# Expert blocks at fixed places, with a scatter that adds weighted rows into the output

## Chip, cores and metric

The kernel runs on one core of one Trainium2 chip. The metric is the device time in microseconds (us), the median over runs; lower is better. Engines are named as in the profile: PE (TensorE), DVE (VectorE), ACT (ScalarE), POOL (GpSimd) and SP (SyncE, which here only issues transfers).

## What is computed

Two layers act on 4 x 32 x 32 tokens of 256 channels, 4096 tokens in all. Layer 0 (a convolution and a state-space scan) is not touched by the change. Layer 1 is an attention without softmax and then a mixture of 16 experts, of which each token uses two:

```python
t = t + _L1_attn_ref(_ln_t(t), ...)
t = t + _L1_ffn_ref(_ln_t(t), ...)

def _L1_ffn_ref(x, gate_w, gate_b, w1, w2, w3):      # 256 -> 512 -> 256, 16 experts
    probs = jax.nn.softmax(einsum('bsd,de->bse', x, gate_w) + gate_b, axis=-1)
    top_probs, top_idx = jax.lax.top_k(probs, 2)
    top_probs = top_probs / jnp.sum(top_probs, axis=-1, keepdims=True)
    dispatch = jnp.sum(one_hot(top_idx, 16) * top_probs[..., None], axis=-2)
    hidden = silu(einsum('bsd,edh->bseh', x, w1)) * einsum('bsd,edh->bseh', x, w2)
    expert_out = einsum('bseh,eho->bseo', hidden, w3)
    return einsum('bseo,bse->bso', expert_out, dispatch)
```

So there are 8192 pairs of a token and an expert. With the given inputs the experts get 411, 318, 424, 490, 591, 836, 278, 654, 596, 645, 718, 547, 389, 510, 475 and 310 of them. In blocks of 128 rows (each expert's last block partly empty) that is 73 blocks. Every expert fills or begins at least three, and 25 blocks lie beyond the third of their expert.

## The kernel before

All matrices are float32. The kernel works in four stages.

**Layer 0** takes the first 2720 us or so. It ends on POOL's products `h<-h,cb_n` and DVE's scans.

**Attention** (about 2720 to 2970 us) works through four batches of 8 tiles of 128 tokens. The program is written under a manual schedule: the source order is the order on each engine. In the loop over `o` the work of batch `o` is interleaved with the first part of batch `n = o + 1` and with the gating of batch `z = o - 1`. `out(o, i)` finishes tile i of batch `o` in `t_all`, which holds all 4096 rows of the residual in SBUF. `expert_in(o, half)` normalises four tiles and stores them in `xd` in DRAM. `turn_e` transposes them on PE, `gates` multiplies by the gate weights, and `turn_g` turns the scores back to rows. `route(z)` is a generator: `on_with(steps, n)` runs its next n steps of DVE work in gaps between other work. It picks the two experts (`hot_all`), their weights (`wts`), counts pairs by expert (`counts`), and gives each pair its block within the expert (`within`) and a one-hot code of its place in that block (`qh`). For the last batch this runs with nothing beside it.

**Ordering** (about 2979 to 3001 us). From the final counts each expert gets as many blocks as it needs, one expert after the other: `end` and `first` are the bounds, `eid` the expert of each of up to 79 blocks. Comparisons of every pair's block with all 79 block numbers, and 64 PE products with `qh` (L1742), list for each slot which pair sits in it. From that come `src` (the row of `xd` to gather) and `dst` (the row of `yd` to write; pair 2t + k is row 2t + k, and empty slots go to spare rows).

**Experts** (about 3002 to 3443 us). `blocks_of(0, NFULL)` runs a fixed number of blocks, 74. A branch runs five more if the counts need them. For each block, `fetch_in` reads the expert's number from `eid` on SP (`value_load`), loads `w1` and `w2` (512 KB each) and issues POOL's indirect gather of 128 rows; `fetch_out` loads `w3`. Both run four blocks ahead. `turn_rows` transposes the rows, `hidden` makes two halves of the hidden layer, and `result` multiplies by `w3`. `put_result` copies PSUM to `yb` on DVE, and POOL scatters it:

```python
            yb = ffn.tile([P, C], F32, name="yb", bufs=4)
            nc.vector.tensor_copy(yb, on["pf", i])
            nc.gpsimd.indirect_dma_start(
                yd[:, :], bass.IndirectOffsetOnAxis(dst[:, i : i + 1], 0), yb, None
            )
```

All scatters write one tensor, so the framework makes each wait for the one before. An expert's weights are loaded again for each of its blocks.

**Final sum** (about 3443 us to the end). `yd` is read back in eight parts of 1 MB, DVE adds both rows of each token times their weights to `t_all` (L1879), and ACT's queue stores the output.

Of the kernel before, what the change touches and what calls it, by code (L numbers as in the profile page):

```python
# [16 lines left out]
P = 128  # L17
# [16 lines left out]
def conv_ssm_attn_moe_kernel(ctx: ExitStack, tc: tile.TileContext, a: dict, out: bass.AP):  # L34
# [19 lines left out]
    NBLK = 2 * NB * L // BS + NE - 1  # L54
    assert 2 * NS == P
# [1048 lines left out]
    wts = l1.tile([P, 2, NTA], F32, name="wts")  # L1104

    t_all = l1.tile([P, NTA, C], F32, name="t_all")
    xd = dram.tile([NB * L, C], F32, name="xd")

    yd = dram.tile([2 * NB * L + P, C], F32, name="yd")
# [4 lines left out]
    groups_f = l1.tile([P, NTA], F32, name="groups_f")  # L1114

    places = l1.tile([P, BS], BF16, name="places")
    blocks_h = l1.tile([P, NBLK], BF16, name="blocks_h")

    groups = l1.tile([P, NTA], BF16, name="groups")
    part_pk = l1.tile([P, 2], F32, name="part_pk")  # L1120
    spare = l1.tile([P, 1], F32, name="spare")
# [11 lines left out]
    def constants(first):  # L1133
# [6 lines left out]
        if first:  # L1140
            count(iota, NE, NE)
            make_upper_triangular(nc, before, 1.0, diag=False)
            count(places_f, BS, 0)
            count(blocks, NBLK, 0)
            count(groups_f, NTA, 0)
            count(part_pk, 2, 1, 1, 2)
            count(spare, 1, 2 * NB * L + 1, 1, 1)
            count(block_p, 1, 0, 1, 1)
        else:
            nc.vector.memset(every, 1.0)  # L1150
            nc.vector.memset(keep, 1.0)
            nc.vector.memset(keep[:, :, 0:1], 0.0)
            nc.vector.tensor_copy(places, places_f)
            nc.vector.tensor_copy(blocks_h, blocks)
            nc.vector.tensor_copy(groups, groups_f)

    with tc.tile_pool(name="wa", bufs=1) as wa, tc.tile_pool(name="att", bufs=1) as att, \
# [4 lines left out]
        tbs = [t_all[:, b * NT : (b + 1) * NT, :] for b in range(NB)]  # L1162
        for i in (0, HT):
            nc.sync.dma_start(out=tbs[0][:, i : i + HT, :], in_=rows(td, 0)[:, i : i + HT, :])
# [101 lines left out]
        def fourth(b, i):  # L1266
            on = batch[b]
            junk = sm.tile([P, C], F32, name="junk", bufs=1)
            nc.scalar.activation(
                junk, on["sq"][:, i, 0, :], AF.Square, accum_out=on["q4"][:, i : i + 1]  # L1270
            )
# [124 lines left out]
        def expert_in(b, half):  # L1396
# [14 lines left out]
            nc.sync.dma_start(out=rows(xd, b)[:, lo:hi, :], in_=on["xe"][:, lo:hi, :])  # L1411
# [24 lines left out]
        def route(b):  # L1436
# [18 lines left out]
            first = sm.tile([P, NT], F32, name="first")  # L1455
            hot = [h[:, b * NT : (b + 1) * NT, :] for h in hots]
            for k, top in enumerate((m1, m2)):
# [7 lines left out]
                nc.vector.tensor_reduce(first, cand, AX.X, ALU.min)  # L1465
                yield
                nc.vector.tensor_tensor(hot[k], cand, over_last(first, NE), ALU.is_equal)
# [19 lines left out]
            for k, top in enumerate((m1, m2)):  # L1487
                nc.vector.tensor_tensor(
                    wts[:, k, b * NT : (b + 1) * NT], top, both, ALU.mult
# [31 lines left out]
            )  # L1521
            yield
            for k in range(2):
# [4 lines left out]
                yield  # L1528

# [32 lines left out]
        for o in range(NB):  # L1562
# [24 lines left out]
            turn_next(0)  # L1587
            v_out(o, 0)
# [70 lines left out]
            if n is not None:  # L1659
                fourth(n, NT - 1)  # L1660
                k2(n, 1)
            out(o, 5)
# [5 lines left out]
            out(o, 7)  # L1668
            if n is None:
# [14 lines left out]
    eid = l1.tile([1, NBLK], I32, name="eid")  # L1684

    used_i = l1.tile([P, 1], I32, name="used_i")
    NFULL = 2 * NB * L // BS + NE // 2 + 2
    src = l1.tile([P, NBLK], I32, name="src")
    dst = l1.tile([P, NBLK], I32, name="dst")
    wp = ctx.enter_context(tc.tile_pool(name="wp", bufs=6))  # L1690
    with tc.tile_pool(name="rt", bufs=1) as rt, tc.tile_pool(name="rt2", bufs=3) as rt2, \
            tc.tile_pool(name="ps_r", bufs=1, space=PSUM) as ps_r:

        nbi = rt.tile([P, NE], I32, name="nbi")
        nc.vector.tensor_scalar(nbi, counts[-1], float(BS - 1), None, ALU.add)
        nc.vector.tensor_single_scalar(nbi, nbi, BS.bit_length() - 1, ALU.arith_shift_right)
        nb = rt.tile([P, NE], F32, name="nb")
        nc.vector.tensor_copy(nb, nbi)
        end = rt.tile([P, NE], F32, name="end")
        nc.vector.tensor_tensor_scan(end, every[:, :NE], nb, 0.0, ALU.mult, ALU.add)  # L1700
        nc.vector.tensor_copy(used_i, end[:, NE - 1 :])
        first = rt.tile([P, NE], F32, name="first")
        nc.vector.tensor_tensor(first, end, nb, ALU.subtract)

        pick = rt.tile([P, 2 * NTA, NE], F32, name="pick")
        nc.vector.tensor_tensor(
            pick, hot_all.rearrange("p k g e -> p (k g) e"), over_middle(first, 2 * NTA), ALU.mult
        )
        bf = rt.tile([P, 2, NTA], F32, name="bf")
        nc.vector.tensor_reduce(bf.rearrange("p k g -> p (k g)"), pick, AX.X, ALU.add)  # L1710
        bh = rt.tile([P, 2, NTA], BF16, name="bh")
        nc.vector.tensor_tensor(bh, bf, within, ALU.add)

        done = rt.tile([P, NE], F32, name="done")
        nc.vector.tensor_scalar(done, end, block_p, None, ALU.is_le)
        ef = rt.tile([P, 1], F32, name="ef")
        nc.vector.tensor_reduce(ef, done, AX.X, ALU.add)
        pe = ps_r.tile([1, P], F32, name="pe")
        nc.tensor.transpose(pe, ef, ident)
        nc.vector.tensor_scalar(eid, pe[:, :NBLK], float(NE - 1), None, ALU.min)  # L1720

        pgp = ps_r.tile([P, 2, NBLK], F32, name="pgp")
        GC = NTA // 2
        n = 0
        for k in range(2):
            for c in range(NTA // GC):
                gs = slice(c * GC, (c + 1) * GC)
                ih = rt2.tile([P, GC, NBLK], BF16, name="ih", bufs=2)  # L1730
                nc.vector.tensor_tensor(
                    ih, over_middle(blocks_h, GC), over_last(bh[:, k, gs], NBLK), ALU.is_equal
                )
                both = rt2.tile([P, GC, 2, NBLK], BF16, name="both", bufs=2)
                nc.vector.tensor_tensor(
                    both[:, :, 0, :], ih, over_last(groups[:, gs], NBLK), ALU.mult
                )
                nc.scalar.activation(
                    both[:, :, 1, :], ih, AF.Copy, scale=part_pk[:, k : k + 1]
                )  # L1740
                for j in range(GC):
                    nc.tensor.matmul(  # L1742
                        pgp.rearrange("p s n -> p (s n)"), qh[:, k, c * GC + j, :],
                        both[:, j, :, :].rearrange("p s n -> p (s n)"),
                        start=(n == 0), stop=(n == 2 * NTA - 1),
                    )
                    n += 1
        low = rt.tile([P, NBLK], F32, name="low")
        nc.vector.tensor_copy(low, pgp[:, 1, :])
        pm = rt.tile([P, NBLK], F32, name="pm")  # L1750
        nc.vector.scalar_tensor_tensor(
            pm, pgp[:, 0, :], 2.0 * P, low, ALU.mult, ALU.add
        )
        none = rt.tile([P, NBLK], F32, name="none")
        nc.vector.tensor_scalar(none, pm, 0.0, None, ALU.is_equal)
        row = rt.tile([P, NBLK], F32, name="row")
        nc.vector.scalar_tensor_tensor(row, none, spare, pm, ALU.mult, ALU.add)
        nc.vector.tensor_scalar(dst, row, -1.0, None, ALU.add)
        both = rt.tile([P, NBLK], I32, name="both_i")
        nc.vector.tensor_scalar(both, pm, 1.0, -1.0, ALU.max, ALU.add)  # L1760
        nc.vector.tensor_single_scalar(src, both, 1, ALU.arith_shift_right)

    with tc.tile_pool(name="ffn", bufs=2) as ffn, \
            tc.tile_pool(name="ps_x", bufs=2, space=PSUM) as ps_x, \
            tc.tile_pool(name="ps_h", bufs=4, space=PSUM) as ps_h, \
# [3 lines left out]
        on = {}  # L1772

        def fetch_in(i):

            e = nc.sync.value_load(eid[0:1, i : i + 1], min_val=0, max_val=NE - 1)
            on["e", i] = e
            for name in ("w1", "w2"):
                t = wp.tile([P, CK, HID], F32, name=name)
                nc.sync.dma_start(  # L1780
                    out=t,
                    in_=a["L1_ffn_" + name][bass.ds(e, 1)].rearrange("o (k p) h -> p (o k) h", p=P),
                )
                on[name, i] = t
            t = ffn.tile([P, C], F32, name="xb", bufs=6)
            nc.gpsimd.indirect_dma_start(  # L1786
                t, None, xd[:, :], bass.IndirectOffsetOnAxis(src[:, i : i + 1], 0)
            )
            on["xb", i] = t

        def fetch_out(i):
            t = wp.tile([P, HK, C], F32, name="w3")
            nc.sync.dma_start(
                out=t,
                in_=a["L1_ffn_w3"][bass.ds(on.pop(("e", i)), 1)].rearrange(
                    "o (k p) c -> p (o k) c", p=P
                ),
            )
            on["w3", i] = t

        def turn_rows(i):
# [115 lines left out]
```

## Time and profile before

| What | Value |
|---|---|
| median of 3 runs | 3470.42 us (3470.37 to 3471.43) |
| the profiled execution | 3483.06 us, its span 3481.3 us |
| mean granted TensorE clock | 0.978 |
| busy share of the span | PE 92%, DVE 83%, ACT 77%, POOL 77% |
| expert weights | 222 loads of 512 KB, 6.0 us to landing |
| gathers `xb<-xd,src` | 74, 5.5 us to landing |
| scatters `yd<-yb,dst` | 74, 5.2 us to landing |
| read-back `y<-yd` | 8 of 1 MB, 10.3 us to landing |
| first PE work of the experts, last scatter issued | 3008.2 us, 3439.35 us |

A busy share is a mean over stages that have different limits; what the change can do has to be read in the stages it touches. Times within the span are counted from its start. The profiled execution is 12.6 us longer than the median of the runs.

### The profile page before, as it was taken

The numbers are of one execution on the slowest core, as the hardware profiler recorded it, in microseconds if no ns is written. First come the engines' busy times: TensorE is split into PE (matmuls) and PEld (weight loads), VectorE is DVE, ScalarE is ACT, GpSimd is POOL, SyncE is SP. The second block draws the span as 40 slices with busy tenths as digits, with TensorE's granted clock in tenths as the row PEclk, the third lists the DMA queues.
The fourth block names the chain that finished last, engine by engine and source line by source line (L and its number), as shares of the span: only waits on it lengthen the run. The fifth ranks groups of instructions, "written<-read, shape, count | busy, mean of one in ns | idle before, by whom it ended". The sixth has DMA issues, their size and how long they took to land. (4 is left out here: it accounts for less than half of the span.)

```text
span 3481.3 us, 62766 instructions
## 1 busy us (share of the span) xinstructions
PE 3205.9 (92%) x23081; PEld 2718.2 (78%) x23081; DVE 2875.8 (83%) x3290; ACT 2680.8 (77%) x4525; POOL 2690.4 (77%) x1185
## 2 busy tenths in 40 slices
PE   7989999999999999999999999889999889699995
PEld 4677877888888888878888887778777666598994
DVE  4799999999999999999999999999999676422224
ACT  1799999998999899989999998999999454221211
POOL 0489988998999899989998999999999532133331
PEclk9999999999999999999999999999999999799997
DMA  3422222222332222223222223222212100699996
GB/s 102 110 61 67 65 64 70 70 72 63 77 74 63 69 76 72 63 64 79 74 68 68 69 65 75 60 62 66 61 62 69 56 19 19 235 325 307 322 308 227
DMA packets 413577, 347.81 MB, mean 100 GB/s; under 512 B 193345, under 2 KB 299841, under 8 KB 413266
## 3 DMA queue, kind: packets, MB, share of 16 engines
q1 hardware_dynamic: 393794, 319.97, 31.9%
q0 software_dynamic: 7104, 19.41, 1.7%
q10 hardware_dynamic: 12368, 4.37, 0.5%
q8 instruction: 185, 3.03, 0.4%
q14 instruction: 126, 1.03, 0.1%
HBM read 313.65 MB, written 29.47 MB: 99 GB/s over the span
## 5 line engine op out<-in xcount | busy, mean ns | idle before, releaser
L934 POOL TENSOR_TENSOR h<-h,cb_n 128x2048 f32<-128x2048 f32 x512 | 2145.2, 4198 | 139.3 <-DVE h L927 69.2
L901 ACT ACTIVATE da<-dt,l_conv_a_log_sb 128x512 f32<-128x512 f32 x2048 | 1434.6, 712 | 76.6 <-DVE h L927 74.4
L948 PE MATMUL y<-ident,h 128*128 128x128 f32 x8192 | 1236.3, 274 | 2.5 <-POOL h L934 2.5
L927 DVE TENSOR_TENSOR_SCAN h<-da,last,ps 128x512 f32<-128x512 f32 x1024 | 1218.5, 1266 | 19.5 <-PE ps L913 11.1
L927 DVE TENSOR_TENSOR_SCAN h<-da,ps 128x512 f32<-128x512 f32 x1024 | 1163.5, 1199 | 55.0 <-PE ps L913 26.5
L881 ACT ACTIVATE bx<-dtxT,proj 128x512 f32<-128x512 f32 x1650 | 1172.5, 711 | 22.4 <-DVE dtxT L576 16.4
L913 PE MATMUL ps<-ident,bx 128*128 128x128 f32 x6600 | 1073.1, 275 | 34.4 <-DVE h L927 18.8
L948 PEld LDWEIGHTS y<-ident,h 128*128 128x128 f32 x8192 | 967.4, 142 | 3.2 <-POOL h L934 3.2
L913 PEld LDWEIGHTS ps<-ident,bx 128*128 128x128 f32 x6600 | 791.1, 142 | 141.5 <-DVE h L927 58.5
L913 PE MATMUL ps<-ident,bxp 128*128 128x128 f32 x976 | 290.7, 298 | 78.6 <-DVE h L927 64.6
L1823 DVE TENSOR_TENSOR hT<-s,p 128x256 f32<-128x256 f32 x148 | 62.4, 422 | 340.9 <-ACT s L1822 340.9
L913 PEld LDWEIGHTS ps<-ident,bxp 128*128 128x128 f32 x976 | 137.0, 140 | 223.5 <-DVE h L927 107.4
L1817 PE MATMUL p<-xT,w 128*128 128x128 f32 x2368 | 292.2, 277 | 0.5 <-ACT xT L1806 0.5
L1817 PEld LDWEIGHTS p<-xT,w 128*128 128x128 f32 x2368 | 285.7, 194 | 4.9 <-ACT xT L1806 0.9
L1837 POOL DMA_INDIRECT yd<-yb,dst x74 | 73.0, 987 | 269.2 <-DMA yd<-yb,dst 172.3
L908 PE MATMUL ps<-dgb,dtxT 128*128 128x128 f32 x1232 | 261.2, 294 | 17.9 <-DVE h L927 12.0
L908 PEld LDWEIGHTS ps<-dgb,dtxT 128*128 128x128 f32 x1232 | 195.6, 191 | 94.7 <-DVE h L927 53.3
L1822 ACT ACTIVATE s<-p 128x256 f32<-128x256 f32 x148 | 56.9, 384 | 276.1 <-PE p L1817 276.1
L405 PE MATMUL bg<-pad,dgc 128*128 128x512 f32 x432 | 221.8, 595 | 3.5 <-DMA dgc<-diags 3.0
L892 POOL TENSOR_SCALAR bxp<-dtxT,proj 128x512 f32<-128x512 f32 x244 | 170.8, 700 | 59.2 <-DVE dtxT L576 59.2
L1829 PE MATMUL pf<-w,hT 128*128 128x256 f32 x592 | 153.3, 382 | 0.1
L1786 POOL DMA_INDIRECT xb<-xd,src x74 | 71.9, 972 | 97.8 <-DMA w<-in_L_ffn_w_dram 73.8
(308 smaller groups left out, 2351.0 us busy)
## 6 DMA issues: line engine op xcount, KB each, us to landing
cb_n<-cd SPq DMA_DIRECT2D x512, 256.0 KB, 3.2
w<-in_L_ffn_w_dram SPq DMA_DIRECT2D x222, 512.0 KB, 6.0
dgc<-diags SPq DMA_DIRECT2D x84, 192.0 KB, 3.2
dgb<-diag_b SPq DMA_DIRECT2D x154, 64.0 KB, 3.1
y<-yd SPq DMA_DIRECT2D x8, 1024.0 KB, 10.3
last<-h SPq DMA_DIRECT2D x256, 2.0 KB, 2.8
diag_b<-zero SPq DMA_DIRECT2D x2, 2048.0 KB, 9.3
xd<-xe SPq DMA_DIRECT2D x8, 512.0 KB, 2.9
```

What stands on the lines that cost most here:

```text
L405: nc.tensor.matmul(made["bg"].rearrange("p (h w) -> p h w", w=WW), made["dgc", m * 3 + i][:, j, :], pads[m][:, half * ROWS + i : (half + 1 ...
L881: nc.scalar.activation(t, made["dtxT", u][:, j, :], AF.Copy, scale=made["proj", u][:, j, R + n : R + n + 1])
L892: nc.gpsimd.tensor_scalar(t, made["dtxT", u][:, 0, :], made["proj", u][:, 0, R + n : R + n + 1], 1.0, ALU.mult, ALU.mult,)
L901: nc.scalar.activation(t, made["dt", u][:, m, :], AF.Exp, scale=A[:, m, n : n + 1])
L908: nc.tensor.matmul(t[:, blk(j, P)], made["dtxT", steps[s][0]][:, j, blk(m, P)], made["dgb", s], start=True, stop=True,)
L913: nc.tensor.transpose(t[:, blk(j, P)], made["bx", s, j][:, blk(m, P)], ident)
L927: nc.vector.tensor_tensor_scan(h[:, m, 1:], made.pop(("da", s, m)), made.pop(("dbx", s, m)), 0.0 if seg == 0 else last[b][:, n, m : m + 1] ...
L934: nc.gpsimd.tensor_tensor(h[:, :, :BANK], h[:, :, 1:], over_middle(made["c", s], DK), ALU.mult)
L948: nc.tensor.matmul(made["y", u][j][:, blk(m, P)], made["h", s][:, m, blk(j, P)], ident, is_transpose=True, start=n == 0 and m == 0, stop=n ...
L1817: nc.tensor.matmul(p12[:, j, s, :], on[w, i][:, ck, blk(h + j, P)], on["xT", i][:, ck, :], start=(ck == 0), stop=(ck == CK - 1),)
L1829: nc.tensor.matmul(on["pf", i], on["hT", i][:, hk, :], on["w3", i][:, hk, :], start=(hk == 0), stop=(hk == HK - 1),)
L1837: nc.gpsimd.indirect_dma_start(yd[:, :], bass.IndirectOffsetOnAxis(dst[:, i : i + 1], 0), yb, None)
```

## The change

Each expert now owns three fixed blocks (`FIX = 3`, 48 in all), numbered `s * 16 + e`, whatever the counts. Only blocks beyond an expert's third are ordered from the counts; there is room for 60 (`NMORE`), and 25 (`NFULL`) of them run always. If more are needed, a branch runs the other 35.

- **Routing.** `route` itself now lists the slots of the fixed blocks, batch by batch, into `found`: a comparison with 48 block numbers, products with the token group and part, and 16 PE products with `qh`. `src` of the fixed blocks follows from `found` by five small operations (`sources`).
- **Ordering beside the experts.** `dst` (`spare_rows`), the bounds (`more_places`) and the slots of further blocks (`more_rows`) are steps of generators that `blocks_of` advances twice in each block.
- **Weights once.** The fixed blocks run expert by expert, and an expert's `w1`, `w2` and `w3` are loaded once for its three blocks, without a value load. Further blocks still load their own set. They are spread among the fixed ones from the thirteenth on.
- **Scatter that adds.** Each finished batch of `t_all` is stored to the output at once, from ACT's queue. `put_result` multiplies the rows by their weights, and POOL's indirect transfer adds them to the output rows. `yd` and the final sum are gone. The weights travel with the rows: `xd` is two columns wider, and SP stores `wts` into these.
- **Empty slots.** They gather a row of zeros (a new row block of `xd`, written first of all on SP's queue from a tile that POOL clears), and add it to a row of a token that is not in the block: for a fixed block one that does not use the expert (`nonmembers`, `count_them`, `place_them` and `list_them`, run on POOL and PE during attention).
- **Buffers.** The weights have three buffers for fixed and three for further blocks instead of six; `p12` in PSUM has three instead of four.

The core of the diff, with parts left out:

```diff
-    NBLK = 2 * NB * L // BS + NE - 1
+    FIX = 3
+    NFIX = FIX * NE
+    NMORE = 2 * NB * L // BS - 2 * (FIX - 1)
+    NBLK = NFIX + NMORE
...
+        none = sm.tile([P, C + 2], F32, name="none_t", tag="junk", bufs=1)
+        nc.gpsimd.memset(none, 0.0)
+        nc.sync.dma_start(out=xd[NB * L :, :], in_=none)
...
+                nc.sync.dma_start(
+                    out=rows(xd, b)[:, :, C:], in_=wts[:, b * NT : (b + 1) * NT, :]
+                )
...
+            at = sm.tile([P, 2, NT], BF16, name="at")
+            nc.vector.scalar_tensor_tensor(
+                at, within[:, :, gs], float(NE), own, ALU.mult, ALU.add
+            )
...
+            nc.vector.tensor_tensor(
+                ih, over_middle(blocks_h[:, :NFIX], 2 * NT),
+                over_last(at.rearrange("p k g -> p (k g)"), NFIX), ALU.is_equal,
+            )
+            yield
+            nc.vector.tensor_tensor(
+                code[:, :, 0, :], ih,
+                over_last(groups[:, b, :, :].rearrange("p k g -> p (k g)"), NFIX), ALU.mult,
+            )
+            for k in range(2):
+                nc.scalar.activation(
+                    code[:, blk(k, NT), 1, :], ih[:, blk(k, NT), :], AF.Copy,
+                    scale=part_pk[:, k : k + 1],
+                )
...
+            for k in range(2):
+                for i in range(NT):
+                    nc.tensor.matmul(
+                        pf.rearrange("p s n -> p (s n)"), qh[:, k, b * NT + i, :],
+                        code[:, k * NT + i, :2, :].rearrange("p s n -> p (s n)"),
+                        start=(k + i == 0), stop=(k == 1 and i == NT - 1),
+                    )
...
+        def place_them():
...
+            for g in range(2):
+                for e in range(NE):
+                    nc.gpsimd.tensor_scalar(
+                        at[:, g, e, :], places_f, rank[:, g, e : e + 1], 1.0,
+                        ALU.is_equal, ALU.mult,
+                    )
+
+        def list_them():
+            pt = ps_b.tile([P, NE], F32, name="pt_r", tag="po")
+            for e in range(NE):
+                for g in range(2):
+                    nc.tensor.matmul(
+                        pt[:, e : e + 1], batch[0]["at"][:, g, e, :], names_h[:, g : g + 1],
+                        start=(g == 0), stop=(g == 1),
+                    )
+            nc.scalar.copy(table, pt)
...
             out(o, 7)
+            nc.scalar.dma_start(out=rows(of, o), in_=tbs[o])
...
+        def fetch(key):
+            c, e = key
+            if c < NFIX:
+                if c < NE:
+                    load("", e, slice(e, e + 1))
+            else:
+                e = nc.sync.value_load(
+                    eid[0:1, c - NFIX : c - NFIX + 1], min_val=0, max_val=NE - 1
+                )
+                load("m", ("more", c), bass.ds(e, 1))
+            t = ffn.tile([P, C + 2], F32, name="xb", bufs=6)
+            nc.gpsimd.indirect_dma_start(
+                t, None, xd[:, :], bass.IndirectOffsetOnAxis(src[:, c : c + 1], 0)
+            )
...
-            nc.vector.tensor_copy(yb, on["pf", i])
+            nc.vector.tensor_scalar(yb, on["pf", key], on["wt", key], None, ALU.mult)
             nc.gpsimd.indirect_dma_start(
-                yd[:, :], bass.IndirectOffsetOnAxis(dst[:, i : i + 1], 0), yb, None
-            )
+                of[:, :], bass.IndirectOffsetOnAxis(dst[:, c : c + 1], 0), yb, None,
+                compute_op=ALU.add,
+            )
...
+        fixed = [(s * NE + e, e) for e in range(NE) for s in range(FIX)]
+        more = [(NFIX + i, None) for i in range(NFULL)]
...
+        blocks_of(todo, chain(spare_rows(), more_places(), more_rows(0, NFULL)))
+        used = nc.values_load(used_i[0:1, 0:1], min_val=1, max_val=NMORE + 1)
+        with tc.If(used > NFULL + 1):
+            for _ in more_rows(NFULL, NMORE):
+                pass
+            blocks_of([(NFIX + i, None) for i in range(NFULL, NMORE)])
-    with tc.tile_pool(name="fin", bufs=4) as fin:
...
```

## The prediction

> **What bounds the kernel now.** I read the forty slices first, then the busy time by stretch, the timelines of the expert stage's two ends, the waits, and the chain that ended last.
>
> The slices show where the change acts. TensorE (PE) is at 9 tenths for most of the span; the DMA engines are lightly used until the last fifth, where they also reach 9. That fifth is the expert stage, after which PE stops.
>
> ```profile
> PE   7989999999999999999999999889999889699995
> DMA  3422222222332222223222223222212100699996
> ```
>
> The waits in that stage, and scatters on GpSimd's timeline (start, duration, idle before): the scatter of block i waits until that of block i-1 has landed, 172.3 us in all, and gathers queue behind it. PE itself waits little.
>
> ```profile
> POOL yd L1837 <- DMA yd<-yb,dst: 172.3, 47, 6.3
> PE px L1804 <- DMA xb<-xd,src: 12.8, 14, 3.2
> ...
> 3411.45 0.99 POOL L1837 DMA_INDIRECT yd<-yb,dst  x1 [4.13 <-DMA yd<-yb,dst]
> ...
> 3414.67 0.99 POOL L1837 DMA_INDIRECT yd<-yb,dst  x1 [0.96 <-DMA yd<-yb,dst]
> ...
> 3417.86 0.99 POOL L1837 DMA_INDIRECT yd<-yb,dst  x1 [0.93 <-DMA yd<-yb,dst]
> ```
>
> From 3411 on the weight loads are over (DMA share 0.23 in that stretch, against 0.90 over the loop) and scatters that wait for each other follow at 3.19 us. Between the first scatter (3019.64) and the last (3439.35) lie 73 steps, 5.75 us each. PE's own floor is lower. Where nothing is late, the copies `yb` on VectorE (DVE) come at even distances:
>
> ```profile
> 3018.93 0.42 DVE L1836 COPY yb<-pf 128x256 f32<-128x256 f32 x1
> ...
> 3024.45 0.42 DVE L1836 COPY yb<-pf 128x256 f32<-128x256 f32 x1
> ...
> 3029.98 0.42 DVE L1836 COPY yb<-pf 128x256 f32<-128x256 f32 x1
> ```
>
> That is 5.52 us. So the loop is PE-bound, with 73 x (5.75 - 5.52) = 16.8 us lost to late gathers. Around the loop PE does nothing useful: from the last attention routing (2970.97) to the first gather (3002.05), then to the first transpose (3008.18); and from the last scatter to the end. The timeline of that start, then the chain's tail (start, duration):
>
> ```profile
> 2970.97 0.29 DVE L1439 TENSOR_TENSOR pr<-pg,l_ffn_gate_b_row 128x128 f32<-128x128 f32 x1 [4.40 <-PE pg L1434]
> ...
> 2987.18 2.86 DVE L1731 TENSOR_TENSOR ih<-blocks_h,bh 128x1264 bf16<-128x1264 bf16 x2
> ...
> 3002.05 1.21 POOL L1786 DMA_INDIRECT xb<-xd,src  x1 [73.79 <-DMA w<-in_L_ffn_w_dram]
> ```
> ```profile
> 3439.35 4.02 DMA yd<-yb,dst
> ...
> 3443.77 5.53 DMA y<-yd
> ...
> 3462.22 11.44 DMA y<-yd
> ```
>
> The tail reads 8 MB of `yd` back, weighs and adds it, and writes 4 MB.
>
> **What the Trainium skill says.** "DMA: Bandwidth & Descriptors", in Rules for kernel authors, says that an accumulating DMA reads its destination and writes later, so another write to the same bytes in between is lost, and the earlier DMA's semaphore must be waited for. So the scatters stay a chain; the chain on `yd` (172.3 us) is the same kind. The same page, Anatomy of one DMA (SWDGE path), gives a fixed cost of about 2.0 us, mostly the receipt of the write; the 3.19 us spacing, 1 us of it issue, agrees. Under Latency and other measured facts it puts one HBM access at 0.2 us on average and 2 us at high load: my price for the added read. No accumulating transfer is in this trace.
>
> **The change part by part.** The profiled execution took 3483.06 us (span 3481.3), 12.6 over the median of 3470.42. I sum against the profiled one and carry the difference over.
>
> *Block count and branch.* Routing the reference's inputs gives 278 to 836 tokens an expert: 73 blocks of 128, 25 past each expert's third. The trace has 74 scatters, the old fixed count. The new program runs 48 + 25 = 73 unconditionally, so exactly enough.
>
> *Loop.* 73 blocks have 72 steps: 72 x 5.52 = 397.4 against 419.7, -22.3. Weights fall from 222 loads to 123 (16 + 25 experts' sets of three; 64.5 MB against 116.4), so mean DMA load about halves: gathers should arrive in time. Added on PE beside the blocks: 64 bf16 products (L2037) at 84 ns (32 of L1742 in 2.68 us at the loop's start) and four transposes, 6.0. ScalarE's and DVE's share (eight 128x200 codes, `choices`, two tiny products a block) hides in their idle time: DVE is busy 92 of 420 us in the loop. If that cover fails, `hT` is late; PE reaches it some 1.5 us after it is ready. Bursts of weights will still delay some scatters: +4. Loop: **-12.3**, if scatters keep pace.
>
> *Do they?* A plain scatter lands in 5.2 us (median of the DMA issues) under full load, spacing 3.19 with little load; halfway gives 4.2. The read adds 0.2 to 2.0 by the skill's price, at 1.1: 5.3 per step, under 5.52. Bounds 4.4 to 6.2. Below zero I exclude: the same rows are written and a read is added. GpSimd's queue has nothing else but gathers (1.27 us a block).
>
> *End.* From the last scatter, 41.95 us become landing 4.0 + 1.1 and 0.5 to stop: **-36.3**. Read-back, weighing and the final stores go; the weight moves into `put_result`, the base rows into four 1 MB stores on ScalarE's queue (L1763) at each batch's end. ScalarE waits there for `out(o, 7)`; what is queued behind it waits for PE transposes later anyway. Nothing.
>
> *From routing to first gather.* Removed: the whole ordering (four 1.47 us comparisons, four products, 64 PE products, a pick and reduce of 1.22 each). Added to `route`: `at`, one comparison and one product on 128x768 (1.47 x 768/1264 = 0.9 each), two codes on ScalarE beside `qh`, 16 PE products after it (1.3), `found`, five small operations of `sources`. After the scan at 2978.68 (+7.7) I count 4.0 chain to `qb`, 0.2 + 1.8, 2.4 for `qh`, 1.1 for the second half of PE's products, 1.6 for the rest: gather at +18.8 instead of +31.1, **-12.3**. Expert weights no longer wait for `eid` but for the attention pools' last reader, `gates(3, 1)` on PE, and start before `wts` goes out on SP behind 3 MB of them (9 us at 340 GB/s); it lands at about +12, before the gather needs it. With loads done, gather to transpose falls from 6.1 to 3.5: **-2.6**.
>
> *Ahead of it.* `list_them` puts 32 products before `out(3, 5)` on PE, 2.7. The 16 products of batch 2 now stand before `gates(3, 0)` and wait for DVE's `code` and `qh` (done at 2966.6 now, 2 us later then) and ScalarE's codes behind `xe`; `gates`, `turn_e` and `gates` (2960.5 to 2969.9 now, overlapped with `xe`) come after in a row: 6.8. Together **+9.5**, bounds +4 to +13. Earlier batches: 2 x 1.3 and three small products on PE (1), DVE's 4.5 in its idle third; SP's first `xd` store waits for a GpSimd memset behind the last `h` product (2722.7), so `t_all` loads go 5 us later than 2718.37, nearly hidden because `root` waits for ScalarE's `yT` copy until 2733.8 (0 to 5, at 0.4). The 32 GpSimd comparisons (0.25 each from a quarter of L892's 0.70) have 16 us until `list_them`. **+4**, bounds 0 to +9.
>
> Sum: -12.3 - 36.3 - 12.3 - 2.6 + 9.5 + 4 = -50. Profiled 3433; median **3420**.
>
> **Rivals.**
> 1. *The accumulating scatter sets the pace* (slower). Place: GpSimd L1926. With spacing s, the loop is 72 x s, its PE additions hidden. The gain without stalls or additions is 60, so it decides at 5.52 + 60/72 = 6.35 us. At 7.0: 3470 - 60 + 107 = 3517. For it: 172.3 us of scatter waits already, steps of 5.75. Against: weights halve, and 3.19 when unloaded. At 6.2, the priced upper end, 3459: still faster.
> 2. *The branch runs.* One more block than 25, and 35 more blocks follow: 35 x 5.52 = 193 more, about 3615. Expert 13 holds 510 tokens, two below a new block; rounding would have to move three its way. Little speaks for it.
> 3. *The front does not shrink*: `list_them`, `pf` and the weights' wait cost their upper bounds (+13, +9) and loads collide with the gathers: 3432.
> 4. *It doesn't do what it says*: 73 blocks at the old 5.75 because gathers wait for other reasons: 72 x 0.23 = +13 in place of +4, 3429.
>
> **How the numbers follow.** Main case with 3 and 4: 0.68. Scatter pace between 5.6 and 6.35, up to 3470: 0.13. Above it: 0.15; branch: 0.03. What is left stands within 0.2%, about what a measurement of this kernel can tell from no change. Faster 0.80, same 0.02, slower 0.18. Favourable bounds (front -9.5, no burst loss -4, read 0.2) give 3405, so low is 3402; the high end goes to 3466, taking in 6.2 us per step and part of the front's excess, leaving out some 0.18 above.
>
> **What would show it.** Right: no `y<-yd`; 73 scatters about 5.5 to 5.6 us apart, PE's slices at 9 through the loop at half the DMA; first gather about 2 us earlier or equal; the end some 6 us after the last scatter. Wrong: scatters waiting for scatters at 6.4 or more, PE waiting for `xb` or `yb` in every block; more than 73 scatters; or the first gather later than 3010.

## Result and profile after

The changed kernel takes **3449.51 us** (median of four runs, 3447.53 to 3451.41) against 3470.93 for the kernel before, run beside it on the same chip (four runs, 3470.37 to 3477.42): ratio 0.9934, 95% interval 0.9917 to 0.9951. That is 21.4 us less; the forecast was 50. The profiled execution took 3450.39 (span 3448.6), close to the median, while the one of the kernel before had been 12.6 above its own.

The forty slices of the changed kernel:

```profile
PE   7999999999999999999999999889999898699997
DMA  3432222223222322233322223222122201367774
```

PE reaches 9 to the end of the loop, and the DMA engines no longer do: mean 186 GB/s in the loop where it was 299. That step went as foreseen. The waits from 3000 us on (engine, tile and line, what it waited for, us in total, times, longest):

```profile
POOL out_dram L1926 <- DMA out_dram<-yb,dst: 78.3, 30, 6.2
POOL out_dram L1926 <- DVE yb L1924: 59.0, 15, 8.6
POOL out_dram L1926 <- DVE wt L1891: 35.2, 13, 4.9
...
PEld px L1880 <- DMA xb<-xd,src: 15.4, 9, 2.9
...
PE px L1880 <- DMA xb<-xd,src: 11.8, 8, 2.5
```

The scatter still waits. A wait for several semaphores is booked on one name: `yb` and `wt` had mostly been ready for a long time, and it was the scatter before that came last. The timelines show it. First GpSimd where the weight loads are over (start, duration, idle before):

```profile
3408.86 1.59 POOL L1926 DMA_INDIRECT out_dram<-yb,dst  x1 [1.68 <-DVE yb L1924]
...
3413.47 1.59 POOL L1926 DMA_INDIRECT out_dram<-yb,dst  x1 [1.73 <-DMA out_dram<-yb,dst]
3418.15 1.57 POOL L1926 DMA_INDIRECT out_dram<-yb,dst  x1 [3.10 <-issue]
...
3433.43 1.55 POOL L1926 DMA_INDIRECT out_dram<-yb,dst  x1 [4.64 <-DVEq L2098]
3437.92 1.55 POOL L1926 DMA_INDIRECT out_dram<-yb,dst  x1 [2.94 <-issue]
```

An accumulating scatter takes GpSimd 1.59 us (a plain one 0.99), and two that wait for each other stand 4.6 us apart (3.19). The last one starts at 3437.92, although DVE's last `yb` begins at 3428.74:

```profile
3428.74 0.48 DVE L1924 TENSOR_SCALAR yb<-pf,wt 128x256 f32<-128x256 f32 x1 [0.96 <-PE pf L1917]
```

The scatters are **9.2 us behind** their rows when the loop's arithmetic is over. DVE's copies in the middle, two stretches of the same timeline:

```profile
3079.85 0.48 DVE L1924 TENSOR_SCALAR yb<-pf,wt 128x256 f32<-128x256 f32 x1
3085.37 0.48 DVE L1924 TENSOR_SCALAR yb<-pf,wt 128x256 f32<-128x256 f32 x1
...
3239.96 0.48 DVE L1924 TENSOR_SCALAR yb<-pf,wt 128x256 f32<-128x256 f32 x1
3246.27 0.48 DVE L1924 TENSOR_SCALAR yb<-pf,wt 128x256 f32<-128x256 f32 x1 [0.83 <-DMA out_dram<-yb,dst]
3253.69 0.48 DVE L1924 TENSOR_SCALAR yb<-pf,wt 128x256 f32<-128x256 f32 x1
```

From the tenth block up to 3240 blocks come at 5.52 us, PE's floor as before; from there on a good third of the steps are longer (6.31, then 7.42 here). Now and then `yb` itself waits for a scatter to free its buffer (three times, 1.6 us in all).

The start, answering to the one shown of before (routing's `pr`, the first gather, the first transpose), and the tail of the chain:

```profile
2978.81 0.29 DVE L1452 TENSOR_TENSOR pr<-pg,l_ffn_gate_b_row 128x128 f32<-128x128 f32 x1 [6.60 <-PE pg L1447]
...
2998.47 1.24 POOL L1868 DMA_INDIRECT xb<-xd,src  x1 [46.70 <-issue]
...
3001.62 0.66 PE L1880 MATMUL px<-ident,xb 128*128 128x128 f32 x2 [6.08 <-issue]
```
```profile
3433.43 1.55 DMA out_dram<-yb,dst
3434.98 2.73 issue
...
3437.92 1.55 POOL out_dram L1926
```

From routing to first gather it is 19.7 us (was 31.1), and to the first transpose 3.2 more (was 6.1). No `y<-yd` is left; from the last scatter to the end it is 10.7 us.

### The profile page after: what moved, and what is told of

Its sections match the earlier page's. It is cut to its first block, busy times and chain, and to the rows that moved or that the text cites. A ratio compares the mean times of both kernels' runs of the same rounds, so it can differ in the third digit from the quotient of the medians.

```text
span 3448.6 us, 62238 instructions
## 1 busy us (share of the span) xinstructions
PE 3203.6 (93%) x23146; PEld 2716.8 (79%) x23146; DVE 2880.5 (84%) x3431; ACT 2682.1 (78%) x4537; POOL 2759.4 (80%) x1220
## 5 line engine op out<-in xcount | busy, mean ns | idle before, releaser
L884 ACT ACTIVATE bx<-dtxT,proj 128x512 f32<-128x512 f32 x1650 | 1173.8, 712 | 22.1 <-DVE dtxT L579 16.3
L1926 POOL DMA_INDIRECT out_dram<-yb,dst x73 | 116.1, 1590 | 230.8 <-DMA out_dram<-yb,dst 78.3
L1902 PE MATMUL p<-xT,w 128*128 128x128 f32 x1536 | 189.6, 277 | 0.6 <-ACT xT L1882 0.6
L1902 PEld LDWEIGHTS p<-xT,w 128*128 128x128 f32 x1536 | 184.4, 194 | 3.1 <-ACT xT L1882 1.0
L1301 POOL TENSOR_TENSOR ksq<-k 128x1024 f32<-128x1024 f32 x8 | 15.1, 1892 | 109.9 <-ACT k L1298 102.1
```

The source lines that it names most:

```text
L884: nc.scalar.activation(t, made["dtxT", u][:, j, :], AF.Copy, scale=made["proj", u][:, j, R + n : R + n + 1])
L1902: nc.tensor.matmul(p12[:, j, s, :], w_of(w, key)[:, ck, blk(h + j, P)], on["xT", key][:, ck, :], start=(ck == 0), stop=(ck == CK - 1),)
L1926: nc.gpsimd.indirect_dma_start(of[:, :], bass.IndirectOffsetOnAxis(dst[:, c : c + 1], 0), yb, None, compute_op=ALU.add,)
```

## Experiments

Two quantities are read from every trace. The **lag** of a block is the start of its scatter minus the start of its `yb`. **Late blocks** are the net sum by which the steps between `yb` exceed 5.52 us, from the tenth step to the last but one; shorter steps count against longer ones, which matters in e3 alone (the first nine steps hold the added ordering work on PE, 5.3 to 5.6 us in all in every changed kernel). Times in us:

| kernel | median | late blocks | largest lag | lag of last block | first to last scatter | last scatter to end |
|---|---|---|---|---|---|---|
| before, second trace (e5) | 3470.09, one run | 12.4 | 18.4 | 0.7 | 413.7 | 41.3 |
| changed | 3449.51 | 13.9 | 18.5 | 9.2 | 423.3 | 10.7 |
| e1 changed again | 3450.24 | 13.0 | 18.9 | 8.4 | 421.7 | 10.8 |
| e2 plain scatter | 3425.98 | 0.0 | 3.8 | 0.8 | 401.2 | 8.9 |
| e3 gathers 8 ahead | 3444.79 | 1.6 | 20.5 | 13.3 | 415.2 | 10.6 |
| e4 few weights | 3428.67 | 0.0 | 2.2 | 1.5 | 402.2 | 11.0 |
| e6 no branch | 3444.30 | 14.9 | 19.5 | 7.3 | 422.5 | 7.2 |
| e7 paced weights | 3445.90 | 9.1 | 18.5 | 9.3 | 418.8 | 10.8 |
| e8 early count | 3450.74 | 13.0 | 18.2 | 8.4 | 421.7 | 10.9 |
| e9 order only | 3443.56 | 6.4 | 18.3 | 9.7 | 416.4 | 10.9 |
| e10 order, free rows | 3431.78 | 0.0 | 6.7 | 2.4 | 402.7 | 12.1 |

e1 to e4 ran on one chip beside before at 3473.92, e5 to e8 beside 3476.73, e9 and e10 beside 3477.30 (medians of 7 or 8 runs). The medians of the changed kernels are of four runs, five for e8, and single runs of one changed kernel lie up to 12.5 us apart: a difference of 5 us between two medians is a hint, one of 18 is not chance.

Theory A: the chain of accumulating scatters is slower, under the weight loads, than PE's 5.52 us. It falls behind block by block; then gathers, which stand in the same queue, and the four `yb` buffers make PE go at the chain's pace. Theory B: only the lookahead of the gathers is too short.

**e1, the changed kernel again.**

> The changed kernel unaltered, as the base for the other runs on this chip and for a second trace. All theories: 3449.5, within 2.5 us. Blocks in the loop at 5.52 us where nothing is late, some 5 us of added PE work in the first nine blocks, 10 to 18 us of late blocks from about the 40th on, the scatters 13 to 18 us behind their rows there and 8 to 10 us behind at the end, and 10 to 11 us from the last scatter to the end.

Measured 3450.24 (3441.26 to 3452.91), ratio to before 0.9920 (0.9896 to 0.9944). Lag and late blocks repeat. Over blocks 21 to 64 scatters start 6.0 us apart, which is the chain's pace. It can be followed link by link in the trace: in 68 of the 72 steps a scatter starts 0.74 to 0.80 us after the one before it has landed, so a step is a landing (5.2 us in the mean of these blocks) and 0.8. The lag passes 10 us at block 34 and 16 at block 38, and late blocks begin with the 42nd step (6.93 us).

**e2, plain scatter.**

```
             nc.gpsimd.indirect_dma_start(
                 of[:, :], bass.IndirectOffsetOnAxis(dst[:, c : c + 1], 0), yb, None,
-                compute_op=ALU.add,
             )
```

> The scatter overwrites in place of adding: the residual and one of the two expert contributions are left out of the output. Theory A (the chain of accumulating scatters is slower under weight loads than PE's 5.52 us a block; it falls behind until the four yb buffers and the four gathers ahead are used up, and then sets the pace): issue falls from 1.59 to 0.99 us, the unloaded spacing from 4.6 to 3.2, the scatters never get more than 8 us behind, the 14 us of late blocks fall to under 4 and the 8 to 9 us of backlog at the end to 1: 3429 to 3433. Theory B (gathers come late only because four blocks of lookahead in GpSimd's queue are too few, the kind of scatter doesn't matter): late blocks stay at 10 to 14 us and only the backlog goes: 3440 to 3444.

Measured 3425.98 (3425.62 to 3428.34), ratio 0.9857 (0.9840 to 0.9874): 24 us less than e1; that is 3 us below the range of A, and far outside that of B. The DMA issues of e1, then of e2 (out<-in, count, median us from issue to landing), and the stretch from 3050 to 3200 of both (busy times of the engines, then PE's clock, DMA share, GB/s):

```profile
out_dram<-yb,dst POOLq DMA_INDIRECT x73, 4.5
```
```profile
out_dram<-yb,dst POOLq DMA_INDIRECT x73, 2.5
```
```profile
3050.00:3200.00 150.00, 147.93 (x1142) 140.45 (x1141) 45.45 (x156) 31.31 (x82) 67.06 (x52) 1.00 0.75 209
```
```profile
3050.00:3200.00 150.00, 147.93 (x1142) 140.43 (x1140) 45.48 (x156) 31.27 (x82) 51.76 (x53) 1.00 0.63 209
```

The same work moves the same 209 GB/s, but with addition the DMA engines are busy 0.75 of the time against 0.63, and the median scatter lands 2.0 us later. A chain adds up means and not medians: over blocks 21 to 63 the mean landing is 5.19 against 3.83 us, so addition costs 1.4 us a scatter. The unloaded spacings, 4.6 and 3.19, differ by the same 1.4. Of this, 0.6 is the longer issue on GpSimd, which is part of the time to landing.

**e3, gathers eight ahead.**

```
+                    while got < min(n, i + AHEAD + 1 + max(0, min(4, i - 9))):
+                        gather(todo[got])
+                        got += 1
```
(`gather` is the second half of `fetch`, its `xb` with `bufs=10` in place of 6.)

> The rows of a block are gathered eight blocks ahead in place of four (ten xb buffers in place of six) from the tenth block on; weights and scatters as before. Theory A: the scatters end when their own chain ends, so nothing is gained but a little of the tail; PE's waits for xb become waits for a free yb: 3446 to 3450. Theory B: the 14 us of late blocks go, PE ends 12 us earlier, and the scatters follow: 3437 to 3441.

Measured 3444.79 (3443.52 to 3449.00): just under what A gave and well above B. The net late blocks went, from 13.0 to 1.6 (the longer steps alone still make 11.3, since `yb` waits for its buffers, but shorter ones make up for them), and the lag of the last block grew from 8.4 to 13.3: what PE gained it handed to the chain. The waits of e3 show the next limit of A, the `yb` buffers:

```profile
DVE yb L1927 <- DMA out_dram<-yb,dst: 36.8, 15, 4.8
```

So the short lookahead is how the delay reaches PE, not where it comes from.

**e4, few weights.**

```
-                e = nc.sync.value_load(...)
-                load("m", ("more", c), bass.ds(e, 1))
+                for name in ("w1", "w2", "w3"):
+                    weights[name, ("more", c)] = weights[name, weights["last"]]
```

> The 25 further blocks load no weights of their own but multiply by the set that was loaded last, so 48 weight loads of 512 KB are left of 123 (their part of the output is then of the wrong expert); no register reads of the expert number on SP either. Theory A with the weight bursts as what stretches the chain: scatters follow at 4.6 to 5.2 us, never more than 6 us behind but for the start, no late blocks after the first nine, backlog at the end under 2: 3427 to 3432. If the accumulation itself is slow whatever else moves (the rival within theory A): spacing stays near 5.9 and the time within 4 us of 3449. Theory B: fewer late gathers too, but the scatter chain isn't the reason: backlog stays above 10 us in the middle.

Measured 3428.67 (3426.99 to 3430.39), ratio 0.9862 (0.9845 to 0.9880). The scatters still add, yet no block is late and the lag stays at 2.2 or less. The landing of the scatters, and the stretch as above:

```profile
out_dram<-yb,dst POOLq DMA_INDIRECT x73, 3.8
```
```profile
3050.00:3200.00 150.00, 147.63 (x1141) 140.19 (x1139) 45.61 (x156) 31.01 (x82) 68.10 (x54) 1.00 0.47 111
```

Both are needed for the shortfall, the addition and the weights beside it; taking away either one frees the loop.

**e5, the kernel before again.**

> The kernel before, unaltered, for a second trace of it; its profiled run of the prediction was 12.6 us above the median. If that excess sat in the loop of the experts (chain of plain scatters under heavier loads, falling behind more in one execution than in another): a run nearer to 3471 has 8 us or more less between first and last scatter than the 419.7 us of the first trace, and the rest within 3 us. If it sat in the stages before: the first transpose of the experts comes 8 us or more earlier than 3008.2 and the loop takes 419.7 within 3 us.

Measured 3470.09, span 3468.2, 13.1 us less than the first trace. Neither: 6.0 us are in the loop (413.7 against 419.7), and the first transpose comes 6.0 earlier (3002.20 against 3008.18), 5.2 of it already at the end of layer 0 (last `ysb` at 2720.04 against 2725.25). Its lag and late blocks are those of the changed kernel: the kernel before, too, was held to the pace of its scatters, plain but beside 299 GB/s (5.7 us a step). Link by link it is the same chain: in 69 of 73 steps here, and in 71 of 73 of the first trace, a scatter starts 0.74 to 0.80 us after the one before has landed. Its lag vanishes only in the last, unloaded stretch, where they are 3.19 us apart:

```profile
3404.21 0.99 POOL L1837 DMA_INDIRECT yd<-yb,dst  x1 [0.93 <-DMA yd<-yb,dst]
...
3407.40 0.99 POOL L1837 DMA_INDIRECT yd<-yb,dst  x1 [0.94 <-DMA yd<-yb,dst]
```

**e6, no branch.**

```
-        used = nc.values_load(used_i[0:1, 0:1], min_val=1, max_val=NMORE + 1)
-        with tc.If(used > NFULL + 1):
-            ...
```

> The conditional part after the loop is left out: no count of used blocks is read by the engines and no block beyond the 25 further ones exists (with these inputs it is not entered). If reading and comparing the count is what makes the tail 10.7 us in place of 5.6: 3443 to 3446 and 5 to 7 us from the last scatter to the end. If the tail is the last accumulating scatter and GpSimd's drain of its queue: 3448 to 3451 and a tail of 9 us or more.

Measured 3444.30 (3436.80 to 3448.71), inside the range for the count; from the last scatter to the end 7.2 us against 10.8.

**e8, count read early.**

```
+        def read_used():
+            used.append(nc.values_load(used_i[0:1, 0:1], min_val=1, max_val=NMORE + 1))
+            yield
         blocks_of(
-            todo, chain(spare_rows(), more_places(), more_rows(0, NFULL)))
+            todo, chain(spare_rows(), more_places(), more_rows(0, NFULL), read_used()))
```

> Only the reading of the count of used blocks is moved, from behind the last block to behind the additions of the first nine; the conditional part stays. If the reading (not the branch itself) is on the path of the tail: 2 to 4 us less, 3445 to 3448, and the tail under 9 us. If the tail is the scatter and the drain, or the branch itself: 3448 to 3451. [...]

Measured 3450.74 (3442.80 to 3452.16), tail 10.9 us, unchanged, as expected if the branch itself or the last scatter makes the tail. With e6: the conditional part, though not entered, goes with 3.6 us of the tail, and where the count is read does not matter. In e2 the tail is 1.9 shorter without the addition. What makes up the 7.2 us that e6 keeps was not taken apart further.

**e7, paced weights.**

```
+            def some(i):
+                first = True
+                while plan and (plan[0] <= i + 2 or (first and plan[0] <= i + 4)):
+                    plan.pop(0)
+                    next(jobs)
+                    first = False
```
(Each step of `jobs` issues one load with `nc.scalar.dma_start`; `some(i)` stands behind both calls of `hidden` in a block.)

> The same 123 weight loads, but all after those of the first four blocks are issued on ScalarE's queue, mostly one behind each of its activations (two a block, two to four blocks ahead of use), in place of sets of three and more at a time on SP's. Same bytes, same load on average. Theory A with bursts as what stretches a scatter: scatters at 5.5 us or less in the loop, late blocks under 4 us, backlog at the end under 4: 3430 to 3437. If the mean load counts and not the bursts: spacing stays near 5.9 where it lags, 3446 to 3452. If ScalarE's issues make hT late: PE waits for hT, above 3452.

Measured 3445.90 (3440.62 to 3449.32). The spread shrank: over blocks 21 to 64 the longest step between scatters fell from 9.85 us in e1 to 7.55. The mean step hardly fell, 5.95 against 6.00, nor did the mean landing there, 5.14 against 5.19. The median over the whole loop even rose, from 4.5 to 4.9:

```profile
out_dram<-yb,dst POOLq DMA_INDIRECT x73, 4.9
```

So, with e4, it is the mean load and not its bursts that stretches the chain.

**e9, order only, and e10, order and free rows.** The order of both:

```
-            if i >= LEAD:
+            if i >= LEAD and i % FIX == FIX - 1:
                 upto = NFULL * (i + 1 - LEAD) // (NFIX - LEAD)
```

and in `put_result` of e10 alone (`put` is the scatter just issued, `before` the last one with its block; not where no gather stands between the two):

```
+            if before is not None and on['between'] and c < NFIX and before[0] + NE == c:
+                tc.declare_no_dep(put.ins, before[1], reason="rows of one expert are distinct")
```

> Only the order of the blocks: the three fixed blocks of an expert stand in a row and the further blocks come after every third one, two or so at a time, in place of singly between them. Same blocks, loads and waits. Theory A: the chain of scatters is as long as before, 3447 to 3453 (weights come in larger groups, so if anything 1 to 3 us more).

> The same order, and the scatter of an expert's second fixed block no longer waits for that of its first, nor that of the third for the second (it still waits for the first, whose rows its padding may name): the rows are distinct, at least while every expert has 256 tokens as here. Four block latencies are left in the chain of about five blocks, 24 us at 6 each against PE's 27.6. Theory A, the chain of landings sets the pace: lag under 9 us through the middle, late blocks after the ninth under 4 us in sum, backlog at the end 2 to 6: 3428 to 3436. Rival A2, the GpSimd's issue and the DMA rings themselves are full (a scatter that needn't wait lands just as much later): 3445 to 3452 with the lag at 16 us as before.

e9 measured 3443.56 (3439.93 to 3448.70), 3 us below its range, with half the late blocks of e1 but the same lag; why the order alone helps a little was not followed up. e10 measured **3431.78** (3419.70 to 3432.17), ratio 0.9860 (0.9839 to 0.9880), inside what A gave and far from A2. The scatters of one expert and the next in e10, on GpSimd's timeline:

```profile
3279.97 1.59 POOL L1927 DMA_INDIRECT out_dram<-yb,dst  x1 [6.93 <-DVE yb L1925]
...
3285.59 1.59 POOL L1927 DMA_INDIRECT out_dram<-yb,dst  x1 [2.74 <-DVE yb L1925]
...
3288.78 1.59 POOL L1927 DMA_INDIRECT out_dram<-yb,dst  x1 [0.30 <-issue]
...
3291.97 1.59 POOL L1927 DMA_INDIRECT out_dram<-yb,dst  x1 [0.30 <-issue]
...
3298.59 1.59 POOL L1927 DMA_INDIRECT out_dram<-yb,dst  x1 [3.74 <-issue]
```

The one at 3285.59 is an expert's first; its second and third now go out 3.19 us after the one ahead, with a gather between as GpSimd's only other work, and the next further block, which still waits, 6.62 us after the third. So the lag falls back in each group, never passes 6.7, and no block is late. In 17 of the 55 steps for which the trace has the landing, a scatter starts 0.3 to 1.4 us before the one ahead has landed; in e1 none does. The DMA traffic and the additions are those of the changed kernel; against e9 only waits were taken out. No run of e9 or of the changed kernel is as fast as its slowest, 3432.17, so it beats the kernel before and the changed one; the 12 us to e9, which has the same order with all waits, are the waits alone. Dropping them rests on every expert having at least 256 tokens, as these inputs give: with fewer, padding of the second block would name rows of the first.

## Why the prediction was right and wrong

The direction was right, and the gain less than half of what was forecast. Its steps are set against two traces that lie near the medians, e5 for before (span 3468.2) and e1 for after (3446.8), 21.4 us apart as the medians are:

| step | forecast | measured |
|---|---|---|
| end of layer 0 (same code in both) | none | 2720.04 to 2722.87: +2.8 |
| from there to routing | +13.5 | 243.7 to 255.6: +11.9 |
| routing to first transpose | -14.9 | 38.5 to 22.9: -15.6 |
| first transpose to first `yb` | none | 10.3 to 12.2: +1.9 |
| first to last scatter | -12.3 | 413.7 to 421.7: +8.0 |
| last scatter to end | -36.3 | 41.3 to 10.8: -30.5 |
| sum | -50 | -21.5 |

**The step that failed is the loop**, and in it the price of a scatter. The forecast put it at 5.3 us, under PE's 5.52: 4.2 for a plain one at half the load, and 1.1 for the read, an estimate midway between the 0.2 and 2.0 us of the Trainium skill (DMA: Bandwidth & Descriptors, Latency and other measured facts). In the runs the chain's pace under load is 6.0, and both terms were too small.

The 4.2 is the middle between 5.2, a landing under full load, and 3.19, a spacing without load. These are two different things: a spacing also holds the 0.8 us from a landing to the next start. The middle of the two spacings, 5.75 and 3.19, is 4.5; with 1.1 that makes 5.6, already above 5.52. The mean landing of e2, 3.8, gives 4.6 for a plain scatter in a chain beside the new load. The addition, 1.1 in the forecast, costs 1.4. It lies between the skill's two figures, but 0.6 of it is the issue on GpSimd, 1.59 in place of 0.99, which the estimate left out. Together 4.6 and 1.4 make the 6.0.

The forecast's own upper end, 6.2, would have been near. It did have this case, a pace between 5.6 and 6.35, and gave it 0.13, where it was the one that came. It also concluded, from a rule that it gives for writes to the same bytes, that all scatters stay in one chain; e10 shows that scatters to distinct rows need not.

What followed from it went two ways. Late blocks: 13.0 us in place of the 4 for bursts, +9.0. And a term that the sum did not have, the lag that is left when PE is done: 8.4 in place of before's 0.7, +7.7, since the unloaded accumulating chain catches up only 5.5 - 4.6 = 0.9 us a block where the plain one had caught up 2.3. PE's added work was 5.3 against 6.0, and the last step, counted as 5.52, is 3.84. Together: +9.0 + 7.7 - 0.7 - 1.7 = 14.3, which is 421.7 against the forecast's 419.7 - 12.3 = 407.4.

**How a scatter delays PE** can now be worked out. From the `yb` of block k to the transposes of block k+6 are four steps, 22.1 us; the gather of that block stands behind the scatter of block k. At a lag of 16 us, 6.1 are left for the scatter's issue (1.6), the pause (0.3) and the gather's landing (5.0, its median in e1): 6.9. So by this estimate PE begins to wait at a lag of some 15 us, and then cannot be ahead of the chain by more. In e1 PE waits for rows seven times after the start, and each time the scatter ahead of the gather lagged 15.7 to 17.2 us. One case, with block 55's `yb` and its scatter (17.1 us behind), the gather of block 61, and the transposes of block 61:

```profile
3324.95 0.48 DVE L1924 TENSOR_SCALAR yb<-pf,wt 128x256 f32<-128x256 f32 x1
...
3342.05 1.59 POOL L1926 DMA_INDIRECT out_dram<-yb,dst  x1 [1.69 <-DMA out_dram<-yb,dst]
...
3343.95 0.99 POOL L1868 DMA_INDIRECT xb<-xd,src  x1 [0.30 <-issue]
...
3350.27 0.44 PE L1880 MATMUL px<-ident,xb 128*128 128x128 f32 x2 [2.00 <-DMA xb<-xd,src]
```

It is this ceiling that made the chain of before look harmless: PE itself waited little, in before 16.8 us by the forecast's own reading, but the 172.3 us of scatter waits were a queue that was already full. The forecast read the 5.75 us step as PE's 5.52 and some late gathers; it was the chain's pace. (For the kernel before this rests on its lags and landings; no experiment was made on it.)

**The first trace was not a constant 12.6 us above the median.** The forecast carried the excess over unchanged. By e5, a single further trace, 6.0 of it sat in the loop, so of the 12.3 that the floor of 5.52 seemed to save, half was not there in a median run: 8.0 - (-12.3) = 20.3 is 14.3 from the pace and 6.0 from this.

**The tail** was priced as the landing and a stop, 5.6, and is 10.8. The conditional part behind the loop, when not entered, has no term in the forecast; without it the tail is 7.2. The other 1.6 stay open.

**The front was right**, and in its steps nearly so: 19.7 us to the first gather against 18.8, 3.2 to the transpose against 3.5, the stretch ahead +11.9 against +13.5, whose two terms (+9.5 and +4) were not measured apart. The 73 unconditional blocks were as computed, and the branch is not entered. Two figures of the forecast do not come out as given, without consequence: the DMA share from 3411 to 3440 is 0.17 and not 0.23, and its favourable bounds give 3407 and not 3405.

## What to carry to other kernels

When a queue of waiting transfers feeds a loop through a few buffers, measure how far it lags behind its producer, block by block, and compare each start with the landing of the transfer before: a lag that stands still at the depth of the buffers says that the queue sets the pace, even if the bottleneck engine hardly waits. Cutting the traffic beside such a chain gains nothing if the change lengthens its own links as much. When a link is priced, a landing and a spacing must not be mixed, and means count, not medians. Then look for links that needn't exist: here rows of one expert are distinct, and dropping about two waits in five was worth 12 us.

## What the runs showed of the hardware

- An accumulating indirect scatter of 128 rows of 1 KB occupies GpSimd for 1.59 us against 0.99, and waiting ones follow at 4.6 us against 3.19 without load. In the loop the mean landing is 5.19 us against 3.83 (e1, e2, blocks 21 to 63), and from 3050 to 3200 the DMA engines' share is 0.75 against 0.63 at the same 209 GB/s.
- A scatter that waits for the one before starts 0.74 to 0.80 us after that one's landing, plain (e5, 69 of 73 steps) or accumulating (e1, 68 of 72).
- Accumulating scatters with distinct rows were in flight together in e10: issued 3.19 us apart beside the changed kernel's weight traffic, less than their median landing of 4.2 us there.
- The end of layer 0, whose code is the same everywhere, came between 2719.18 and 2725.25 us over the twelve traces, and the kernel before took 3461.00 to 3483.11 us in its runs: between two single traces, a difference of 5 us in a stage need not come from the change.
